# Places of tokens in a mixture of experts: reckoned from scores, by products and scans, with the softmax behind them

## The chip, the core and the metric

The kernel runs on one core of one Trainium2 chip. The time is the device time of one execution in microseconds (us); the number that counts is the median of several executions. Five engines work side by side, each through its own queue in order: PE (TensorE, matrix products; PEld is its loading of weights), DVE (VectorE), ACT (ScalarE), POOL (GpSimd) and SP (SyncE, which here issues most DMAs). SBUF is the on-chip memory of 128 partitions, PSUM the smaller one that PE writes, in banks of 512 fp32 numbers a partition.

## The reference, cut to what matters

Two layers on a batch of 4 images of 384 channels and 32 x 32 places (1024 tokens each). The first layer is a selective scan in four directions, and then a mixture of four experts of which each token uses two; the second is an attention of 8 heads and a two-layer network. The change is in the routing of the experts:

```python
def _L0_ffn_ref(x, gate_w, gate_b, w1, b1, w2, b2):
    scores = jnp.einsum('bsd,de->bse', x, gate_w) + gate_b
    probs = jax.nn.softmax(scores, axis=-1)
    topk_vals, topk_idx = jax.lax.top_k(probs, TOP_K)
    mask = jnp.sum(jax.nn.one_hot(topk_idx, NUM_EXPERTS, dtype=probs.dtype), axis=-2)
    masked = probs * mask
    masked = masked / (jnp.sum(masked, axis=-1, keepdims=True) + 1e-09)
    h = jax.nn.gelu(jnp.einsum('bsd,edh->ebsh', x, w1) + b1[:, None, None, :], approximate=False)
    y = jnp.einsum('ebsh,ehd->ebsd', h, w2) + b2[:, None, None, :]
    return jnp.einsum('bse,ebsd->bsd', masked, y)
```

The kernel computes for each token only its two experts. So it needs three things: the *place* of each token's copy in a list that is sorted by expert, the *expert* of each block of that list, and the *gate* (the weight) of each copy.

## The kernel before, in words

**Scan layer.** `scan_layer` goes over 32 units (image, direction, half of the places). For each, `chunk` works in groups: POOL multiplies inputs (L440), ACT makes decays by exp (L449), DVE scans along the places (`tensor_tensor_scan`, L454) and multiplies half of the results (L461), POOL the other half (L468), and PE sums over the states (L475, into `acc`). `project` prepares the next unit beside it (dt_ps L365, `mag` and `lnw` on POOL, L395 and L396). The inputs `dtr` come by DMA from SP's queue (L424). POOL and DVE work in turn on `bx`: six buffers.

**Tail.** When an image's scan is done, its tail is laid beside the scan of the next one. `tail_batch` runs `route`, `first_layer` (`experts`, `combine`, `prologue`) and `second_layer` (`attention`, `last_layers`). The route of image 0 stands by itself; those of images 1 and 2 are the steps `between` of the last layers of images 0 and 1 (L1198), and that of image 3 comes behind the scan (L1383). I call them routes 0 to 3. The tail has high priority at most spots.

**Route.** `spread` turns the tokens, sums the scores `sc` (128 tokens on partitions, 8 blocks of tokens, 4 experts: 128x32) and their statistics, and then calls `places` (L683). Behind it the 16 scatters (L697, indirect DMAs issued by POOL) put each token's row at its place `pos`; `experts` loads the number of the expert of each of 11 blocks into SP's register (L880) and then that expert's weights (L889, L897). The gates are read by `combine` alone (L977), behind all experts.

**`places` before** (L709 to L869), all on 128 partitions, with small operands in one PSUM bank (`area`, by the name `places` in the profile; `small` cuts pieces of it):

- softmax over 4 experts: maximum, difference, exp on ACT (L734), sum, reciprocal, two products (L732 to L738)
- for each pair of experts whether one's probability is above the other's, ties by number (L745 to L748), their sum `number` (L751); `chosen` (first, second; L754), `rank` (either; L755)
- the gates: probability times `rank`, sum, reciprocal, product (L756 to L761)
- two products on PE, with a triangle of ones (`before`) and with ones, count how many tokens ahead of each, and how many in all, chose an expert (L767, L768); a copy brings both from PSUM (L770), and seven adds in a row sum up the blocks (L774), an eighth the totals (L776)
- how many whole pairs of blocks and odd blocks each expert uses (L780 to L795, four adds in a row for where each begins), then the places (L798 to L840)
- the expert of each block, from comparisons of block numbers with where each expert begins (`later`, L846, to L866)
- the gates are picked with the places in one product and one reduction (L832 to L835) and copied (L868).

**The order.** The program is laid out by a planner: the framework simulates the engines' times, and each engine's queue gets its instructions in the order of that simulation, by priority and then by readiness. Nothing near the change is ordered by hand. Within one PSUM bank it keeps PE and DVE from working at once.

Of the kernel before, what the change touches and what calls it, by code (L numbers as in the profile page):

```python
# [12 lines left out]
ALU = mybir.AluOpType  # L13
# [102 lines left out]
class Body:  # L116
# [525 lines left out]
    def spread(self, b, x1, room):  # L642
# [38 lines left out]
        nc.vector.tensor_add(sc, sc, self.bg.unsqueeze(1).to_broadcast([P, MB, NE]))  # L681
# [27 lines left out]
    def places(self, sc, room):  # L709
# [18 lines left out]
        def over(v):  # L728
            return v.unsqueeze(2).to_broadcast([P, nt, NE])

        red, prob = small([P, nt]), small([P, nt, NE])
        nc.vector.tensor_reduce(red, sc, AX.X, ALU.max)  # L732
        nc.vector.tensor_sub(sc, sc, over(red))
        nc.scalar.activation(sc, sc, AF.Exp)  # L734
        nc.vector.tensor_reduce(red, sc, AX.X, ALU.add)
        nc.vector.reciprocal(red, red)
        nc.vector.tensor_mul(prob, sc, over(red))
        nc.vector.tensor_mul(sc, sc, over(red))  # L738

        shape = [P, nt, NE, NE]  # L740
        mine = sc.unsqueeze(3).to_broadcast(shape)
        other = prob.unsqueeze(2).to_broadcast(shape)
        above = room.tile(shape, "g_above", "g_above")
        same = small(shape)
        nc.vector.tensor_tensor(above, other, mine, op=ALU.is_gt)  # L745
        nc.vector.tensor_tensor(same, other, mine, op=ALU.is_equal)
        nc.vector.tensor_mul(same, same, self.lower.unsqueeze(1).to_broadcast(shape))
        nc.vector.tensor_add(above, above, same)  # L748
        rank = room.tile([P, nt, NE], "g_rank", "g_rank")
        number = small([P, nt, NE])  # L750
        nc.vector.tensor_reduce(number, above, AX.X, ALU.add)  # L751
        chosen = small([P, TOP, nt, NE])
        for k in range(TOP):
            nc.vector.tensor_scalar(chosen[:, k], number, float(k), None, op0=ALU.is_equal)  # L754
        nc.vector.tensor_scalar(rank, number, float(TOP), None, op0=ALU.is_lt)  # L755
        nc.vector.tensor_mul(prob, prob, rank)  # L756
        nc.vector.tensor_reduce(red, prob, AX.X, ALU.add)
        nc.vector.tensor_scalar_add(red, red, 1e-9)
        part = room.tile([P, nt], "g_red", "g_red")
        nc.vector.reciprocal(part, red)  # L760
        nc.vector.tensor_mul(sc, prob, over(part))  # L761


        ps = room.bank("p", "cnt_ps")
        n = nt * NE
        flat = rank.rearrange("p m e -> p (m e)")
        nc.tensor.matmul(ps[:, :n], self.before, flat, start=True, stop=True)  # L767
        nc.tensor.matmul(ps[:, n : 2 * n], self.ones, flat, start=True, stop=True)  # L768
        cnt = small([P, 2, nt, NE])
        nc.vector.tensor_copy(cnt.rearrange("p t m e -> p (t m e)"), ps[:, : 2 * n])  # L770
        run = room.tile([P, nt, NE], "g_run", "g_run")
        nc.vector.memset(run[:, 0, :], 0.0)
        for m in range(nt - 1):
            nc.vector.tensor_add(run[:, m + 1, :], run[:, m, :], cnt[:, 1, m, :])  # L774
        total = small([P, NE])
        nc.vector.tensor_add(total, run[:, nt - 1, :], cnt[:, 1, nt - 1, :])  # L776

        ns = nt * P // P
        need = room.tile([P, NE, ns], "g_need", "g_need")
        nc.vector.tensor_tensor(  # L780
            need, total.unsqueeze(2).to_broadcast([P, NE, ns]),
            self.full[:, :ns].unsqueeze(1).to_broadcast([P, NE, ns]), op=ALU.is_gt,
        )

        used = small([P, 2, NE])
        blocks = room.tile([P, NE], "g_blocks", "g_blocks")
        nc.vector.tensor_reduce(blocks, need, AX.X, ALU.add)
        nc.vector.tensor_reduce(used[:, 0], need[:, :, 1::2], AX.X, ALU.add)
        nc.vector.scalar_tensor_tensor(
            used[:, 1], used[:, 0], -2.0, blocks, op0=ALU.mult, op1=ALU.add  # L790
        )
        first = room.tile([P, 2, NE + 1], "g_first", "g_first")
        nc.vector.memset(first[:, :, :1], 0.0)
        for e in range(NE):
            nc.vector.tensor_add(first[:, :, e + 1], first[:, :, e], used[:, :, e])  # L795
        pairs, odd = first[:, 0], first[:, 1]
# [4 lines left out]
        at = cnt[:, 0]  # L801
        nc.vector.tensor_add(at, at, run[:, :nt, :])
        full, back = room.tile([P, NE], "g_full", "g_full"), small([P, NE])
        nc.vector.tensor_scalar(
            back, odd[:, :NE], float(NHALF) - 0.5, -float((NHALF + 2) * P), op0=ALU.is_gt, op1=ALU.mult
        )
        nc.vector.scalar_tensor_tensor(
            back, odd[:, :NE], float(P), back, op0=ALU.mult, op1=ALU.add
        )
        nc.vector.tensor_scalar(  # L810
            full, more.to_broadcast([P, NE]), float(SLOT), float(NFULL * SLOT),
            op0=ALU.mult, op1=ALU.add,
        )
        nc.vector.tensor_add(back, back, full)
        nc.vector.scalar_tensor_tensor(
            back, pairs[:, 1:], -float(SLOT), back, op0=ALU.mult, op1=ALU.add
        )
        nc.vector.tensor_scalar(full, used[:, 0], float(SLOT), None, op0=ALU.mult)
        ends = room.tile([P, nt, NE], "g_ends", "g_ends")
        nc.vector.tensor_tensor(  # L820
            ends, at, full.unsqueeze(1).to_broadcast([P, nt, NE]), op=ALU.is_ge
        )
# [652 lines left out]
```

## Time and profile before

| what | value |
|---|---|
| timed executions | 4278.92, 4278.86, 4291.83 us; median 4278.92 |
| the profiled execution | 4300.74 us; its span 4299.0 us, granted PE clock 0.865 |
| busy in the span | PE 77%, DVE 66%, ACT 59%, POOL 70% |
| route 0: L732 to L868 | 807.75 to 849.46 us |
| route 1 | 1731.29 to 1771.21 us |
| route 2 | 2737.95 to 2781.50 us |
| route 3 | 3483.17 to 3499.03 us |
| POOL's last work of the scan layer ends | 3458 us |

All times in a view of the profile count from the span's start. A row of a group or tile gives the line of the code, the engine, the operation, what it writes and reads, and durations in ns. A row of the waits gives who waited for whom, us in total, how often and the longest. A duration on DVE goes from the start of an instruction to its last write, so neighbours may overlap by some 0.1 us.

### The profile page before, as it was taken

How to read it: one execution, taken by the hardware profiler on the slowest of the kernel's cores; microseconds unless marked ns; L12 is line 12 of the kernel's file. 1: busy time of each engine (PE TensorE's matmuls, PEld its weight loads, DVE VectorE, ACT ScalarE, POOL GpSimd, SP SyncE). 2: the span in 40 equal slices, each digit the busy share in tenths (PEclk: the TensorE clock that was granted, in tenths of full speed). 3: DMA queues.
4: the chain of work that ended last, by engine and by line, in shares of the span. 5: the costliest groups of instructions: out<-in, count | busy, mean ns of one | idle time of the engine just before them, and what ended most of it. 6: DMA issues, size and time to landing. Idle time of an engine off the chain costs nothing. (4 is left out here: it accounts for less than half of the span.)

```text
span 4299.0 us, 45575 instructions
## 1 busy us (share of the span) xinstructions
PE 3329.5 (77%) x13244; PEld 1560.8 (36%) x13244; DVE 2852.0 (66%) x4200; ACT 2516.4 (59%) x4486; POOL 3020.0 (70%) x1471
## 2 busy tenths in 40 slices
PE   6445444389897888589985889579896889998896
PEld 2111111155553223145652223135553225566322
DVE  5998997878786867788786878878887820010101
ACT  5555545556665775666664777666665654343354
POOL 5999997898898968789898978888989810000100
PEclk8666666689998999589997999679998999999997
DMA  5454563577795535578886434558789243345100
GB/s 140 128 124 122 135 170 107 168 220 224 229 276 158 137 113 142 169 207 236 239 257 191 114 101 140 158 173 237 234 236 272 77 158 100 121 143 202 50 26 19
DMA packets 410322, 693.69 MB, mean 161 GB/s; under 512 B 51024, under 2 KB 209616, under 8 KB 410064
## 3 DMA queue, kind: packets, MB, share of 16 engines
q1 hardware_dynamic: 400752, 664.29, 53.4%
q0 software_dynamic: 8192, 25.17, 1.8%
q8 instruction: 106, 1.74, 0.2%
q14 instruction: 152, 1.25, 0.1%
q10 hardware_dynamic: 1120, 1.25, 0.1%
HBM read 569.00 MB, written 121.50 MB: 161 GB/s over the span
## 5 line engine op out<-in xcount | busy, mean ns | idle before, releaser
L440 POOL TENSOR_TENSOR bx<-dtr,bcs 128x1024 f32<-128x1024 f32 x768 | 1791.8, 2358 | 181.1 <-PE acc L475 93.6
L449 ACT ACTIVATE da<-dtr,nega 128x512 f32<-128x512 f32 x1536 | 1045.5, 690 | 928.7 <-DVE bx L461 580.8
L468 POOL TENSOR_TENSOR bx<-bx,bcs 128x1024 f32<-128x1024 f32 x384 | 903.7, 2357 | 154.6 <-DVE carry L465 67.3
L475 PE MATMUL acc<-bx,sel 128*32 128x512 f32 x3072 | 493.5, 701 | 306.4 <-POOL bx L468 261.0
L941 PE MATMUL h_ps<-xc,w 128*128 128x256 f32 (+1 forms) x3168 | 663.5, 365 | 47.7 <-DVE xc L928 17.4
L956 PE MATMUL y_ps<-w,hs 128*128 128x384 f32 x1824 | 644.6, 507 | 52.5 <-ACT hs L949 52.5
L941 PEld LDWEIGHTS h_ps<-xc,w 128*128 128x128 f32 x3168 | 551.2, 198 | 218.9 <-issue 93.7
L454 DVE TENSOR_TENSOR_SCAN bx<-da,carry,bx 128x512 f32<-128x512 f32 x384 | 473.8, 1270 | 114.7 <-ACT da L449 64.4
L454 DVE TENSOR_TENSOR_SCAN da<-da,carry,bx 128x512 f32<-128x512 f32 x384 | 476.1, 1273 | 77.5 <-ACT da L449 62.1
L454 DVE TENSOR_TENSOR_SCAN bx<-da,bx 128x512 f32<-128x512 f32 x384 | 453.7, 1211 | 90.9 <-ACT da L449 54.3
L461 DVE TENSOR_TENSOR bx<-da,bcs 128x512 f32<-128x512 f32 x768 | 509.8, 679 | 3.0
L454 DVE TENSOR_TENSOR_SCAN da<-da,bx 128x512 f32<-128x512 f32 x384 | 455.5, 1219 | 76.5 <-ACT da L449 53.0
L956 PEld LDWEIGHTS y_ps<-w,hs 128*128 128x128 f32 x1824 | 353.0, 197 | 337.4 <-issue 71.7
L1071 ACT ACTIVATE ex<-s_ps 128x512 f32<-128x512 f32 x512 | 300.3, 591 | 164.2 <-PE s_ps L1065 148.4
L1065 PE MATMUL s_ps<-w 64*128 64x512 f32 x1024 | 305.1, 659 | 68.5 <-ACT ex L1071 64.4
L977 POOL TENSOR_TENSOR diag<-ident,g_weight 128x1024 f32<-128x1024 f32 x8 | 15.1, 1903 | 443.1 <-PE xc_ps L924 430.0
L1111 PE MATMUL o_acc<-ex,vt 128*64 128x512 f32 x1024 | 286.1, 638 | 24.6 <-ACT ex L1071 18.5
L946 ACT ACTIVATE hs<-h_ps,bb 128x256 f32<-128x256 f32 (+1 forms) x528 | 199.9, 440 | 174.9 <-PE h_ps L941 170.9
L475 PEld LDWEIGHTS acc<-bx,sel 128*32 128x32 f32 x3072 | 76.2, 116 | 603.9 <-POOL bx L468 373.3
L960 DVE TENSOR_TENSOR y<-y_ps,bb 128x384 f32<-128x384 f32 x76 | 41.6, 548 | 250.6 <-PE y_ps L956 250.6
L365 PE MATMUL dt_ps<-xd,wdt 108*128 108x512 f32 x192 | 123.6, 731 | 73.0 <-ACT mag L404 48.3
L1065 PEld LDWEIGHTS s_ps<-w 64*128 64x128 f32 x1024 | 81.8, 189 | 269.1 <-ACT ex L1071 222.6
(218 smaller groups left out, 3593.3 us busy)
## 6 DMA issues: line engine op xcount, KB each, us to landing
w<-in_w SPq DMA_DIRECT2D x352, 576.0 KB
dtr<-dd SPq DMA_DIRECT2D x1536, 128.0 KB
bcs<-both SPq DMA_DIRECT2D x512, 128.0 KB
dd<-one_e SPq DMA_DIRECT2D x96, 256.0 KB
dd<-mag SPq DMA_DIRECT2D x96, 256.0 KB
rows<-zero SPq DMA_DIRECT2D x76, 192.0 KB
xt<-x SPq DMA_DIRECT2D x32, 384.0 KB
xs<-rows SPq DMA_DIRECT2D x32, 384.0 KB
```

What stands on the lines that cost most here:

```text
L440: pool = nc.gpsimd.tensor_mul(bx, dtr[q][1], bc[:, 0].unsqueeze(1).to_broadcast([P, 2, HF])).ins
L449: nc.scalar.activation(da, dtr[q][0][:, j, :], AF.Exp, scale=nega[:, col : col + 1])
L454: nc.vector.tensor_tensor_scan(run(h), run(da), run(bx[:, j, :]), 0.0 if first else hold, ALU.mult, ALU.add,)
L461: dve = nc.vector.tensor_mul(bx[:, j, :], h, cg).ins
L468: pool = nc.gpsimd.tensor_mul(bx, bx, cg.unsqueeze(1).to_broadcast([P, 2, HF])).ins
L475: nc.tensor.matmul(acc[lo : lo + DB, :], sel, out[q][:, j, :], start=(g == 0), stop=(g == NG - 1),)
L941: nc.tensor.matmul(ps[:, r, :], w1[(f + r) // wf][:, c, (f + r) % wf * P : ((f + r) % wf + 1) * P], xc[:, c, :], start=(c == 0), stop=(c = ...
L946: nc.scalar.activation(hs[:, f + r, :], ps[:, r, :], AF.Identity, bias=bb[:, f + r : f + r + 1])
L956: nc.tensor.matmul(out[:, :D], hs[:, f, t * P : (t + 1) * P], w2[f // wf][:, f % wf, :], start=(f == 0), stop=(f == FC - 1),)
L1065: ins = nc.tensor.matmul(ps, w[rows, j * P : (j + 1) * P], w[rows, halves(i)], start=True, stop=True).ins
L1071: done.append(nc.scalar.activation(ex[:, o, :], ps, AF.Exp, scale=HD**-0.5, accum_out=sums[:, t, 2 * j + o, i : i + 1],).ins)
L1111: ins = nc.tensor.matmul(out[cols, :], made[t][1][:, j, cols], ex[:, o, :], start=(j == 0), stop=(j == MB - 1),).ins
```

## The change

`spread` no longer adds the bias; `places` does. The order of probabilities is the order of the scores, so the comparisons take the scores, and everything that leads to places and experts comes first. The softmax and the gates stand at the end. Where the comparison needs two copies of the scores, one (`score`) is made in PSUM. The count by two products, a copy and nine adds becomes ten products that accumulate in PSUM: their first columns are the places within an expert, the last the totals. The adds in a row for where each expert begins become scans over 16 flags; the scan of the pairs is made twice, once into SBUF and once into PSUM (`again`). Several steps are joined, and several small pieces move between SBUF and PSUM.

```diff
-        nc.vector.tensor_add(sc, sc, self.bg.unsqueeze(1).to_broadcast([P, MB, NE]))
...
+        score = small([P, nt, NE])
+        nc.vector.tensor_add(score, sc, bg)
+        nc.vector.tensor_add(sc, sc, bg)
...
+        above = room.tile([P, nt, NE, 2, NE], "g_above", "g_above")
+        same = small(shape)
+        nc.vector.tensor_tensor(same, other, mine, op=ALU.is_equal)
+        nc.vector.tensor_tensor(above[:, :, :, 0], other, mine, op=ALU.is_gt)
+        nc.vector.tensor_mul(above[:, :, :, 1], same, self.lower.unsqueeze(1).to_broadcast(shape))
+        number = small([P, nt, NE])
+        nc.vector.tensor_reduce(
+            number, above.rearrange("p m e t o -> p m e (t o)"), AX.X, ALU.add
+        )
+        rank = room.tile([P, nt, NE], "g_rank", "g_rank")
+        nc.vector.tensor_scalar(rank, number, float(TOP), None, op0=ALU.is_lt)
+        at, total = small([P, nt, NE]), small([P, 1, NE])
+        lo = used_up[0] - (nt + 1) * NE
+        count = area[:, lo : used_up[0]].rearrange("p (m e) -> p m e", e=NE)
+        nc.tensor.matmul(count[:, 0, :], self.before, rank[:, 0, :], start=True, stop=True)
+        for m in range(nt):
+            nc.tensor.matmul(
+                count[:, m + 1 :, :], self.ones,
+                rank[:, m, :].unsqueeze(1).to_broadcast([P, nt - m, NE]),
+                start=(m == 0), stop=(m == nt - 1), skip_group_check=True,
+            )
+            if m == 0:
+                nc.tensor.matmul(
+                    count[:, 1:nt, :], self.before, rank[:, 1:, :],
+                    start=False, stop=False, skip_group_check=True,
+                )
...
+        need = small([P, 2, NE, nj])
+        nc.vector.tensor_tensor(need, total..., self.full..., op=ALU.is_gt)
+        pairs_sb = room.tile([P, 1 + NE * nj], "g_pairs", "g_pairs")
+        pairs_ps, blocks_ps = small([P, 1 + NE * nj]), small([P, 1 + NE * nj])
+        def sums(out, t):
+            nc.vector.memset(out[:, :1], 0.0)
+            nc.vector.tensor_tensor_scan(
+                out[:, 1:], self.ones[:, : NE * nj], need[:, t].rearrange("p e j -> p (e j)"),
+                0.0, ALU.mult, ALU.add,
+            )
+            return out[:, ::nj]
+        pairs, even = sums(pairs_sb, 1), sums(blocks_ps, 0)
+        odd = small([P, NE + 1])
+        nc.vector.tensor_sub(odd, even, pairs)
+        again = sums(pairs_ps, 1)
+        used = room.tile([P, NE], "g_used", "g_used")
+        nc.vector.tensor_reduce(used, need[:, 1], AX.X, ALU.add)
...
+        row = room.tile([P, nt, 2, NE], "g_row", "g_row")
...
+        chosen = small([P, TOP, nt, NE])
+        for k in range(TOP):
+            nc.vector.tensor_scalar(chosen[:, k], number, float(k), None, op0=ALU.is_equal)
+        picked = room.tile([P, TOP, nt, 2, NE], "g_pick", "g_pick")
+        for t in range(2):
+            nc.vector.tensor_mul(picked[:, :, :, t], chosen, row[:, :, t]...)
+        place = small([P, TOP, nt])
+        nc.vector.tensor_reduce(place..., picked..., AX.X, ALU.add)
+        pos = room.sb.tile([P, TOP, nt], I32, tag="g_pos", name="g_pos", bufs=2)
+        nc.vector.tensor_copy(pos, place)
...
+        ef = room.tile([P, NSLOT], "g_ef", "g_ef")
+        lone, both = later(NHALF, odd, "lone"), later(NFULL + 1, again, "later")
+        half = small([P, NHALF])
+        nc.vector.tensor_reduce(half, lone, AX.X, ALU.add)
+        nc.vector.tensor_reduce(ef[:, : NFULL + 1], both, AX.X, ALU.add)
+        other = room.tile([P, NHALF], "g_half", "g_half")
+        nc.vector.tensor_reduce(other[:, 2:], lone[:, : NHALF - 2], AX.X, ALU.add)
+        nc.vector.tensor_copy(other[:, :2], ef[:, NFULL : NFULL + 1].to_broadcast([P, 2]))
+        nc.vector.tensor_sub(other, other, half)
+        nc.vector.scalar_tensor_tensor(
+            ef[:, NFULL:], other, more, half, op0=ALU.mult, op1=ALU.add
+        )
+        expert = room.sb.tile([P, NSLOT], I32, tag="g_expert", name="g_expert", bufs=2)
+        nc.vector.tensor_copy(expert, ef)
...
         red, prob = small([P, nt]), small([P, nt, NE])
         nc.vector.tensor_reduce(red, sc, AX.X, ALU.max)
         nc.vector.tensor_sub(sc, sc, over(red))
...
+        gates = room.tile([P, TOP, nt, NE], "g_gates", "g_gates")
+        nc.vector.tensor_mul(gates, chosen, sc.unsqueeze(1).to_broadcast([P, TOP, nt, NE]))
+        weight = room.tile([P, TOP, nt], "g_weight", "g_weight")
+        nc.vector.tensor_reduce(weight..., gates..., AX.X, ALU.add)
```

Left out behind `row` are the three steps that fill it: the place in the expert's pairs, whether the token is in the expert's last odd block, and how far off that one lies. In this cut, a "..." within a line stands for the broadcast or rearranged view of the operand.

## The prediction

> **What bounds the kernel now.** I read the page first, for its slices, and then only the four places where `places` runs, since nothing else is edited.
>
> ```profile
> PE 3329.5 (77%) x13244; PEld 1560.8 (36%) x13244; DVE 2852.0 (66%) x4200; ACT 2516.4 (59%) x4486; POOL 3020.0 (70%) x1471
> ...
> PE   6445444389897888589985889579896889998896
> ...
> DVE  5998997878786867788786878878887820010101
> ...
> ```
>
> That fence's slices read so: up to about 3457 us the scan layer runs, and DVE and POOL are busy for seven tenths or more in nearly every slice (POOL's row, not shown, is like DVE's); behind it both are all but idle and PE is at nine tenths. (A slice is 107 us, so the scan fills the first 32.) The scan stage is paced by POOL's products (L440, L468) and the DVE scans between them; the tail by PE.
>
> The table by stretch, one row for each of the four routes, comes next; its columns are the stretch, its length, then busy us (count) of PE, PEld, DVE, ACT, POOL, the granted clock, DMA share and GB/s.
>
> ```profile
> 807.50:849.50 42.00, 9.28 (x38) 2.72 (x38) 40.08 (x100) 19.29 (x33) 23.29 (x11) 0.57 0.40 124
> 1731.00:1771.40 40.40, 23.04 (x74) 6.18 (x78) 35.37 (x99) 23.08 (x34) 27.87 (x13) 0.54 0.33 88
> 2733.50:2781.60 48.10, 21.32 (x58) 4.66 (x58) 43.35 (x98) 25.70 (x39) 36.48 (x17) 0.54 0.33 98
> 3482.60:3499.00 16.40, 13.19 (x73) 5.46 (x70) 11.69 (x68) 9.82 (x25) 0.00 (x0) 1.00 0.23 76
> ```
>
> In the first three DVE is busy 40.1 of 42.0, 35.4 of 40.4 and 43.4 of 48.1 us while POOL is busy only 23.3, 27.9 and 36.5. So for these 130 us of the scan DVE is the pacer and POOL, the pacer elsewhere, waits. The waits of POOL in three windows around them (route 0, 1, 2 in this order) name what it waited for:
>
> ```profile
> POOL bx L468 <- DVE places L754: 7.0, 1, 7.0
> POOL bx L468 <- DVE carry L465: 6.5, 1, 6.5
> ...
> POOL rows L697 <- DVE g_weight L868: 7.4, 1, 7.4
> ...
> POOL bx L468 <- DVE g_ends L823: 5.4, 1, 5.4
> ```
>
> With 2.3 us more for the positions in route 0 (L697) and 1.9 in route 2 (L735) these are 30.5 us in which POOL stood behind this code. That is the most that the change can win in the scan.
>
> Why DVE is slow there is seen in the views of the tiles `g_later`, `g_half`, `g_ef` and `g_full` (min/median/max ns over the four routes):
>
> ```profile
> L846 DVE TENSOR_TENSOR g_later<-slot_at_i,g_first x4: 178/1339/6737, 822.9 to 3495.5; 128x27 f32<-128x27 f32 x4
> L846 DVE TENSOR_TENSOR g_lone<-slot_at_i,g_first x4: 155/158/2358, 823.5 to 3495.6; 128x9 f32<-128x9 f32 x4
> L858 DVE TENSOR_TENSOR g_half<-g_ef,g_half x4: 144/150/2297, 829.4 to 3496.2; 128x2 f32<-128x2 f32 x4
> L861 DVE TENSOR_TENSOR g_half<-g_half x4: 141/153/2369, 831.6 to 3496.2; 128x1 f32<-128x1 f32 x4
> L862 DVE SCALAR_TENSOR_TENSOR g_ef<-g_half,g_more x4: 221/222/2246, 834.0 to 3496.4; 128x3 f32<-128x3 f32 x4
> L866 DVE CAST g_expert<-g_ef x4: 172/173/1198, 837.4 to 3496.7; 128x11 int32<-128x11 f32 x4
> L853 DVE TENSOR_REDUCE g_ef<-g_later x4: 165/166/169, 827.1 to 3495.9; 128x9 f32<-128x27 f32 x4
> ```
>
> Operations on one to 27 elements take 0.14 to 0.22 us when POOL rests and up to 2.4 us (once 6.74) while it multiplies. Only those stretch whose operands are all in SBUF; the reduction (L853), and every line with an operand in `places` (PSUM), keeps its time in all four routes.
>
> **The change, part by part.** Durations are those of one execution of 4300.74 us (span 4299.0); the three timed runs have a median of 4278.92 (to 4291.83), 0.5% below it. I work out differences and take them off the median.
>
> *Operands moved to PSUM.* The new `later` compares read `odd` and `again`, `half` and the last steps have a PSUM operand. Of the two-input lines stretched in routes 0 to 2, this takes L846 (0.69-0.18, 2.36-0.16, 6.74-0.18 and 1.99-0.18), L858 (2.30-0.15), L861 (2.37-0.15) and L862 (2.25-0.22): 0.51+2.20+6.56+1.81+2.15+2.22+2.03 = 17.5 us. The one-input stretches (L866 1.03, L810 0.84) I keep: the expert cast stays in SBUF and a copy of `ef` joins it. Added is one more add with both inputs in SBUF (`score`, its result in PSUM); no row has that form. Bounds: nothing, or 2.3 us each; I take the nearest rows, L680 and L681, which in routes 0 to 2 lost 2.00+1.15 us in six tries, 0.5 each, 1.6 for three. Net -15.9.
>
> The Trainium skill (SBUF — State Buffer, "Who interferes with whom") says that a DVE instruction with two SBUF inputs is blocked by a GpSimd instruction that reads SBUF; it names the inputs and not the result. By it `score` can lose like L846: 3 x 2.3 = 6.9 us rather than 1.6, and the net would be -10.6.
>
> *Fewer instructions.* Before, L681 and the body of `places` are 64 DVE instructions, whose unstretched durations (route 3) sum to 11.7 us; after it they are 51. Priced by the nearest rows: 0.19 for a 32-element step, 0.16 for a 4-element one, 0.29 for one of 128, a 256-element reduction 0.42, and three scans of 16 elements, which no row shows: between 0.16 (L774) and 1.21 (L454 on 512), near the small end, 0.19 (all three 0.5 to 3.6, taken 0.6). Sum 9.6, so -2.2 a route, -6.5 for three.
>
> The skill speaks against it (Perfetto Trace Analysis, "Optimizing Scalar/DVE Operations"): DVE pays about 60 ns to reach SBUF and 125 to reach PSUM, so some 15 steps moved to PSUM would cost 1 us a route. The trace has 0.15 for L804 with its result in PSUM against 0.144 to 0.150 for L858 in SBUF alone; I charge nothing.
>
> *Products for sums.* Two products, a copy (L770) and nine adds become ten accumulating products that leave positions and totals in PSUM. From the time view of route 0, then of route 3:
>
> ```profile
> 815.45 0.61 PE L767 MATMUL cnt_ps<-g_rank,before_i 128*128 128x32 f32 x2 [8.67 <-ACT da L449]
> ...
> 815.87 0.61 PE L768 MATMUL cnt_ps<-g_rank,ones 128*128 128x32 f32 x2
> ```
>
> A product is two instructions, and starts 0.42 us after the one before it (0.24 in route 3, at full clock, from 3490.54 to 3490.78). Eight more are 3.4 us of PE in routes 0 to 2, where PE is busy 9.3 of 42.0, 23.0 of 40.4 and 21.3 of 48.1 us and hides them, and 1.9 in route 3. But the step to `need` now waits for ten products (4.2+0.2 us) where L770 waited for two; behind `need` stand the scans (L454) for which POOL waits. If scans are queued ahead of `need`, as L454 was put between L757 and L758, the wait is free; if not it is 3.4 more. I take 1.0 a route: +3.0.
>
> *Softmax behind.* The 32-element exp (L734) now follows positions and experts. DVE waited for it 0.9, 3.7, 0 and 1.5 us. It still must wait, but for the gates, which only `combine` reads far later. Bounds -4.6 to +4.6 over three routes (an ACT queue deeper at the new spot); I take 0. The scatter (L697), and SP's load of expert numbers (L880, which held SP's queue up to 21.0 us in route 1), are released sooner; the 16 scatters a route still take POOL 1.27 us each (20 us), only sooner, in its queue before products that then come as much later; what queues behind L880 on SP are weights and `dtr` loads, and no wait of POOL in these windows names `dtr`, so I count nothing.
>
> *Route 3.* From L681 to L840 it takes 16.0 us (3482.95 to 3498.94). Without exp and its wait (2.8) and softmax steps the positions come 3 to 4 us sooner, less 1.8 for products. PE is busy 160.0 of the 160 us from 3540 and 149.4 of the next 150: attention of batch 2 fills what the scatter leaves, so 2 us sooner against 1.9 us of PE: 0. Were the cover gone, -4 to +2.
>
> *Sum.* DVE is freed of 15.9+6.5-3.0 = 19.4 us in the three routes, out of POOL's 30.5. Not all comes through: POOL also waited 7.6 us for `acc` (L475) in route 1, and DVE idles 1.9 to 5 us in each. I take three quarters, 15 us. Forecast 4279-15 = **4264 us**.
>
> **Rivals.**
>
> *Products become the wait (slower).* `need` goes straight behind `rank` in DVE's queue, and other PE work, such as the 3.63 us group at L1226, comes between the products, which share one PSUM tile with all DVE steps. DVE then stands 4.4 us and 3.6 for each such group in each of routes 0 to 2, and the scans queued behind it starve POOL. For it: PE's queue holds such groups in routes 1 and 2, at a clock of 0.54. Against: L770 waited 0.4 us at most. It decides from a stand of 7.5 us a route, where 3 x 7.5 eats the 22.4 us freed before products are counted; with two groups between, 4.4+7.3 = 11.7 us, it is 35.1-22.4 = 12.7 too much: **4292**.
>
> *The time freed is not on the path.* POOL's gaps fill with its other waits (L440 for `acc` 93.6 us, for `dtr` 31.0 over the scan), or the scan ends sooner and PE, left with the same attention work, ends when it did. For: PE's nine tenths behind 3457. Against: PE is idle half of each window. **4279**, 4268 to 4290.
>
> *All of it comes.* All 30.5 us of POOL's waits go: **4248**.
>
> *It doesn't do what it says.* The planner orders queues by its own estimate; if the softmax still goes ahead of the positions, only operand places and counts remain: 4264 to 4268, since I gave the softmax's move nothing in the scan; its chance is inside the forecast's.
>
> A new plan also shifts far loads and groups; I allow the spread of the three runs, 13 us, to each side.
>
> **How the numbers follow.** Forecast (4254 to 4272) 0.42, of which 0.32 is faster by over 0.3% (12.8 us, about what a measurement can tell); all of it 0.17; not on the path 0.17; products 0.24. So faster 0.49, same 0.10+0.17 = 0.27, slower 0.24. The range runs from 4240 to 4298: it holds the forecast, the quiet rival, most of both outer ones.
>
> **What would show it.** Right: in routes 0 to 2 no compare or half step above 0.3 us; the three windows shorter by 4 to 10 us, POOL's waits there under 15 us; the tenth product within 5 us of `rank`. Wrong: DVE idle before `need` for over 5 us; `score` stretched to 2 us each time; the windows shorter but the end of POOL's work (3457) unmoved, or that moved and the end not.

## The result, and the profile after

| | before | after |
|---|---|---|
| median (lowest to highest) | 4288.3 us (4278.86 to 4292.33, 6 runs) | 4264.31 us (4256.45 to 4270.68, 6 runs) |
| ratio, 95% interval | 1 | 0.9947 [0.9931, 0.9964] |
| span of the profiled execution | 4299.0 us | 4258.3 us |

The kernel is 24 us faster by the medians, 0.53% by the ratio on record. The forecast was 15 us (0.35%) and 4264. That the time is the one forecast, to 0.3 us, is luck: the kernel before measured 9 us longer here than in the three runs that the forecast started from, and the gain is 9 us more than forecast, and the two cancel.

The page of after, to be set beside the first fence of the prediction:

```profile
PE 3330.8 (78%) x13308; PEld 1572.8 (37%) x13308; DVE 2838.3 (67%) x4148; ACT 2519.7 (59%) x4486; POOL 3020.0 (71%) x1471
...
PE   6445544389887888689996888679986899998896
...
DVE  5999997788877877788877878778877830000101
```

PE has 64 instructions more (32 products, of two instructions each), DVE 52 fewer; the scan still fills 32 slices and PE's nine tenths stand behind it. The table by stretch, again one row for each route from the first step of `places` to the gates (columns: stretch, length, busy us (count) of PE, PEld, DVE, ACT, POOL, clock, DMA share, GB/s):

```profile
804.30:834.60 30.30, 13.87 (x48) 6.55 (x48) 28.46 (x82) 17.94 (x31) 21.33 (x15) 0.56 0.63 188
1718.50:1753.20 34.70, 20.34 (x82) 6.20 (x76) 30.23 (x87) 25.11 (x38) 30.92 (x16) 0.62 0.49 140
2704.00:2731.30 27.30, 18.97 (x68) 7.43 (x68) 20.23 (x61) 20.06 (x30) 14.79 (x12) 0.63 0.44 137
3470.50:3488.00 17.50, 16.56 (x66) 6.13 (x62) 9.01 (x52) 12.33 (x34) 4.51 (x5) 0.80 0.41 112
```

The first three are 11.7, 5.7 and 20.8 us shorter; the prediction asked for 4 to 10. The length of a window isn't the gain, though: in route 2 DVE has 23.1 us less to do in it, of which only 3.3 us are work of `places` (14.27 to 10.95 us); the rest is scan work that now lies outside. The waits of POOL in windows round the first three (waiter, whom it waited for, us in total, times, longest):

```profile
POOL bx L468 <- DVE carry L465: 4.9, 1, 4.9
...
POOL rows L696 <- DVE places L872: 0.2, 1, 0.2
...
POOL bx L468 <- DVE g_back L812: 0.9, 1, 0.9
...
POOL bx L468 <- DVE bx L454: 5.5, 1, 5.5
...
POOL rows L696 <- DVE places L875: 0.3, 1, 0.3
```

Of the 30.5 us that POOL stood behind this code (a `carry` of route 0 among them, 6.5) there are left 11.8: 1.4 us for the code itself, 4.9 us for that `carry`, and 5.5 us for scans of route 2 (L454) that are queued behind the first steps of `places`, which took 2.0 of these 5.5 us. The views of single tiles (min/median/max ns over the four routes) show why:

```profile
L849 DVE TENSOR_TENSOR g_later<-slot_at_i,places x4: 175/175/176, 820.4 to 3481.5; 128x27 f32<-128x27 f32 x4
L862 DVE COPY g_half<-g_ef x4: 144/544/1387, 823.1 to 3482.0; 128x2 f32<-128x2 f32 x4
L863 DVE TENSOR_TENSOR g_half<-g_half,places x4: 132/154/158, 823.2 to 3482.2; 128x3 f32<-128x3 f32 x4
L868 DVE CAST g_expert<-g_ef x4: 163/958/1836, 823.7 to 3482.6; 128x11 int32<-128x11 f32 x4
L733 DVE TENSOR_TENSOR places<-sc,bg x4: 193/195/2282, 804.6 to 3471.1; 128x32 f32<-128x32 f32 x4
```

The compare that had taken up to 6.74 us takes 0.176 at most (L849), the half step beside it 0.158 (L863). What still stretches has all its inputs in SBUF: the copy L862 (0.92 and 1.39 us in routes 1 and 2), the cast L868 (1.75 and 1.84 in routes 0 and 1) and, once, `score` (L733).

**Where the time went.** The scan layer's 32 units end in the same order in both kernels, so the ends of its units (each the end of the unit's last scan, L454) cut the span into comparable stages. Route 0 lies in the ninth unit, route 1 in the 17th and 18th, route 2 in the 19th to 26th. Rows for the ninth unit, the 10th to 16th, and all behind the scan, same columns as above, first of before:

```profile
751.80:888.00 136.20, 53.51 (x200) 24.01 (x197) 107.79 (x216) 61.56 (x100) 112.66 (x63) 0.63 0.58 182
888.00:1662.10 774.10, 679.15 (x2873) 333.15 (x2872) 605.54 (x815) 519.63 (x970) 663.18 (x317) 0.94 0.66 189
...
3435.20:4299.00 863.80, 778.87 (x3144) 387.35 (x3142) 89.20 (x230) 378.45 (x797) 38.38 (x37) 0.95 0.30 102
```

then of after:

```profile
751.10:875.50 124.40, 58.01 (x202) 27.88 (x199) 97.52 (x203) 62.37 (x100) 112.80 (x63) 0.63 0.65 195
875.50:1628.50 753.00, 651.48 (x2777) 318.41 (x2775) 601.35 (x807) 515.40 (x964) 660.35 (x316) 0.94 0.67 191
...
3421.80:4258.30 836.50, 759.56 (x3073) 386.48 (x3071) 88.23 (x217) 363.99 (x755) 39.40 (x38) 0.95 0.31 104
```

In the ninth unit POOL's work is the same (112.7 and 112.8 us) and DVE's is 10.3 us less: the unit is 11.8 us shorter. Here the change itself is at work. The two other rows are something else. No line of the change runs in units 10 to 16, yet they are 21.1 us shorter, and there PE has 96 instructions and 28 us less to do; behind the scan it has 71 instructions and 19 us less. This is work of the tail that has another place in PE's queue: units 17 to 26 hold it, and are 27.0 us *longer* (249.0+883.5 before, 258.7+900.8 after), although routes 1 and 2 in them are shorter. So of the 40.7 us between the two profiles, 11.8 stand in the ninth unit, and most of the rest in stages that differ in which tail work the planner put there. POOL's last work of the scan layer ends at 3445.0 us, 13.0 earlier than before. The experiments ask whether that order is a part of the change's effect or an accident of it.

### The profile page after: what moved, and what is told of

Its sections match the earlier page's. It is cut to its first block, busy times and chain, and to the rows that moved or that the text cites. A ratio compares the mean times of both kernels' runs of the same rounds, so it can differ in the third digit from the quotient of the medians.

```text
span 4258.3 us, 45670 instructions
## 1 busy us (share of the span) xinstructions
PE 3330.8 (78%) x13308; PEld 1572.8 (37%) x13308; DVE 2838.3 (67%) x4148; ACT 2519.7 (59%) x4486; POOL 3020.0 (71%) x1471
## 3 DMA queue, kind: packets, MB, share of 16 engines
q8 instruction: 107, 1.75, 0.2%
## 5 line engine op out<-in xcount | busy, mean ns | idle before, releaser
L440 POOL TENSOR_TENSOR bx<-dtr,bcs 128x1024 f32<-128x1024 f32 x768 | 1793.7, 2362 | 195.6 <-PE acc L475 84.0
L468 POOL TENSOR_TENSOR bx<-bx,bcs 128x1024 f32<-128x1024 f32 x384 | 905.4, 2362 | 132.4 <-DVE carry L465 59.9
L978 PE MATMUL y_ps<-w,hs 128*128 128x384 f32 x1824 | 643.7, 506 | 55.9 <-ACT hs L971 54.9
L454 DVE TENSOR_TENSOR_SCAN bx<-da,carry,bx 128x512 f32<-128x512 f32 x384 | 473.7, 1271 | 134.5 <-POOL bx L440 69.5
L454 DVE TENSOR_TENSOR_SCAN bx<-da,bx 128x512 f32<-128x512 f32 x384 | 452.3, 1210 | 125.4 <-POOL bx L440 69.7
L454 DVE TENSOR_TENSOR_SCAN da<-da,carry,bx 128x512 f32<-128x512 f32 x384 | 475.7, 1274 | 79.5 <-ACT da L449 63.1
L454 DVE TENSOR_TENSOR_SCAN da<-da,bx 128x512 f32<-128x512 f32 x384 | 455.4, 1219 | 67.5 <-ACT da L449 46.8
```

The costliest lines, as they stand in the source:

```text
L440: pool = nc.gpsimd.tensor_mul(bx, dtr[q][1], bc[:, 0].unsqueeze(1).to_broadcast([P, 2, HF])).ins
L454: nc.vector.tensor_tensor_scan(run(h), run(da), run(bx[:, j, :]), 0.0 if first else hold, ALU.mult, ALU.add,)
L468: pool = nc.gpsimd.tensor_mul(bx, bx, cg.unsqueeze(1).to_broadcast([P, 2, HF])).ins
L978: nc.tensor.matmul(out[:, :D], hs[:, f, t * P : (t + 1) * P], w2[f // wf][:, f % wf, :], start=(f == 0), stop=(f == FC - 1),)
```

## The experiments

Four theories are named in the expectations. **S**: what counts are the DVE instructions stretched by POOL, and their end. **N**: fewer instructions and fewer waits. **E**: positions and experts are ready earlier, the softmax being behind. **P**: any edit gives the planner another order of all queues, and that order moves the time. All ratios are to runs of the kernel before on the same chip; after itself was not run again beside the later kernels, so it is compared with them by these ratios.

Since stages can be compared where totals mislead, here are all kernels by stage (us of the profiled execution; units counted from 1) ahead of the single verdicts. Each row is one execution, and stages of one execution scatter: up to 1740 us the queues of PE, ACT and POOL have the same order in before and b_ctl, and (but for the place of one exp on ACT) the same in after, a_ctl2, a_one, a_two and a_blk, yet units 10 to 16 took 774.1 and 781.3 us, and 753.0 to 764.2.

| kernel | ratio, 95% interval | unit 9 (route 0) | 10–16 | 17–18 (route 1) | 19–26 (route 2) | 27–32 | behind the scan |
|---|---|---|---|---|---|---|---|
| before | 1 | 136.2 | 774.1 | 249.0 | 883.5 | 640.6 | 863.8 |
| b_ctl | 1.0063 [1.0044, 1.0081] | 136.2 | 781.3 | 241.5 | 916.1 | 634.4 | 854.8 |
| b_ctl4 | 1.0044 [1.0027, 1.0061] | 134.5 | 772.9 | 240.1 | 914.4 | 636.0 | 861.9 |
| after | 0.9947 [0.9931, 0.9964] | 124.4 | 753.0 | 258.7 | 900.8 | 633.8 | 836.5 |
| a_ctl | 0.9980 [0.9965, 0.9995] | 128.3 | 760.7 | 258.9 | 919.9 | 624.9 | 836.8 |
| a_ctl2 | 0.9996 [0.9987, 1.0006] | 124.2 | 758.4 | 260.2 | 909.8 | 642.8 | 845.9 |
| b_psum | 0.9932 [0.9914, 0.9951] | 128.4 | 758.2 | 244.4 | 873.5 | 643.4 | 855.9 |
| a_sbuf | 0.9955 [0.9937, 0.9973] | 126.6 | 761.0 | 252.2 | 883.3 | 642.8 | 848.7 |
| a_prod | 1.0047 [1.0032, 1.0062] | 130.8 | 766.2 | 253.5 | 892.1 | 648.2 | 868.0 |
| a_smfirst | 1.0051 [1.0038, 1.0065] | 129.6 | 767.2 | 261.9 | 908.7 | 632.7 | 858.1 |
| a_free | 1.0064 [1.0044, 1.0085] | 126.7 | 754.4 | 256.1 | 925.9 | 642.5 | 864.8 |
| a_blk | 0.9978 [0.9967, 0.9990] | 127.3 | 764.2 | 274.9 | 923.7 | 624.2 | 823.1 |
| a_one | 0.9965 [0.9949, 0.9980] | 125.5 | 758.5 | 272.6 | 922.6 | 623.8 | 826.8 |
| a_two | 0.9985 [0.9974, 0.9996] | 131.0 | 757.7 | 272.8 | 926.4 | 625.9 | 829.1 |

**b_psum: the operands alone.** Before, with the compares' and half steps' operands in PSUM, for which the two differences of the half steps become a reduction, a copy and one difference; nothing else of the change.

```diff
+        again = small([P, 2, NE + 1])
+        nc.vector.tensor_copy(again, first)
...
-            ef[:, : NFULL + 1], later(NFULL + 1, pairs, "later"), AX.X, ALU.add
+            ef[:, : NFULL + 1], later(NFULL + 1, again[:, 0], "later"), AX.X, ALU.add
...
-        half = room.tile([P, 2, NHALF], "g_half", "g_half")
...
+        half = small([P, NHALF])
+        lone = later(NHALF, again[:, 1], "lone")
```

> The kernel before with one part of the change alone: the comparisons and half sums of `later` get an operand in PSUM (two more DVE instructions a route). Theory S (what was won is DVE time lost to operations whose inputs all lie in SBUF while POOL works): the stretched rows of L846, L858, L861, L862 vanish (17.5 us in three routes), time 9 to 15 us below the kernel before, ratio 0.9965 to 0.998. Theory N (fewer and earlier instructions won it): no gain, ratio 0.999 to 1.001. Theory P (what was won comes from the new order of the queues that the planner lays out): any ratio from 0.995 to 1.005, without regard to the stretched rows.

Measured 4258.5 us (4252.53 to 4270.18), beside 4290.1 for before. The tile's view:

```profile
L848 DVE TENSOR_TENSOR g_later<-slot_at_i,places x4: 170/171/172, 837.2 to 3459.6; 128x27 f32<-128x27 f32 x4
```

The compare has lost its stretch in all four routes, with POOL as busy as ever. The ninth unit is 6 to 8 us shorter than with the three orders of before, and this at nearly the same order: PE's, ACT's and POOL's queues are those of before up to its 874 us, and DVE's differs only in how the steps of `places` lie between its other work. DVE spent 12.7 us from L681 on in route 0, where it had spent 22.5. POOL still waits 7.0 us in route 0 for L754, the step behind the softmax. As a whole this kernel can't be told from after (the intervals overlap), with none of the products, scans or the move of the softmax.

**a_sbuf: the operands back.** After, with the starts of the experts, `odd` and `half` in SBUF again (and, not in this cut, `wrap` in PSUM).

```diff
-        odd = small([P, NE + 1])
+        odd = room.tile([P, NE + 1], "g_odd", "g_odd")
...
-        lone, both = later(NHALF, odd, "lone"), later(NFULL + 1, again, "later")
-        half = small([P, NHALF])
+        lone, both = later(NHALF, odd, "lone"), later(NFULL + 1, pairs, "later")
+        half = room.tile([P, NHALF], "g_hsum", "g_hsum")
```

> The changed kernel with those operands back in SBUF (`odd`, `half` and the compared starts; same number of instructions). Theory S: the stretched rows are back, 9 to 15 us above the changed kernel, so ratio to the kernel before 0.9965 to 0.998. Theory N: as fast as the changed kernel, 0.994 to 0.996. Theory P: anywhere from 0.990 to 1.000.

Measured 4268.4 us (4262.14 to 4279.82).

```profile
L863 DVE TENSOR_TENSOR g_half<-g_half,g_hsum x4: 145/237/1859, 818.1 to 3471.1; 128x3 f32<-128x3 f32 x4
L864 DVE SCALAR_TENSOR_TENSOR g_ef<-g_half,g_more,g_hsum x4: 205/704/2265, 820.0 to 3471.3; 128x3 f32<-128x3 f32 x4
```

The stretch is back: the time above 0.45 us of each instruction from L680 on sums over routes 0 to 2 to 17.8 us here, against 6.7 in after and 19.4 in before. But no price of it shows. The ratio is what theory N expected and below theory S's range, which its interval reaches; from after's it can't be told (0.9955 against 0.9947). The ninth unit is 2.2 us longer than in after, which is within the 124.2 to 128.3 us of after's three orders.

**b_ctl and a_ctl: the same instructions in another order.** In before the two lines that make `chosen` go behind `rank` (the diff); in after they go up behind `rank` from their place ahead of `picked`.

```diff
+        nc.vector.tensor_scalar(rank, number, float(TOP), None, op0=ALU.is_lt)
...
-        nc.vector.tensor_scalar(rank, number, float(TOP), None, op0=ALU.is_lt)
```

> A control: the kernel before with the two lines of `chosen` moved behind the line of `rank`; the same instructions with the same operands, but another plan of all queues. Theories S and N: within 0.2% of the kernel before. Theory P: off by 0.3% or more, either way.

> A control: the changed kernel with the two lines of `chosen` moved up behind `rank`, ahead of the ten products; the same instructions with the same operands, but another plan. Theories S and N: within 0.2% of the changed kernel, ratio to the kernel before 0.993 to 0.997. Theory P: off from that by 0.3% or more, either way.

Measured 4319.15 us (4311.43 to 4322.09) and 4284.26 us (4272.95 to 4292.73), beside 4290.1. An exchange that changes no work costs before 0.63% and after 0.33%. In the traces, 3993 of PE's 13244 places and 339 of POOL's 1471 hold something else in b_ctl than in before, and 5644 of 13308 and 385 of 1471 in a_ctl than in after. The ninth units move by 0 and 3.9 us; most of what moves is behind.

**a_free and a_blk: twenty more compares a route,** in after, with one operand in PSUM and with both in SBUF.

```diff
+        extra = room.tile([P, NFULL + 1, NE - 1], "g_extra", "g_extra")
+        for _ in range(20):
+            nc.vector.tensor_tensor(extra, self.slot_at..., again[:, 1:NE]..., op=ALU.is_ge)
```

(`pairs` in place of `again` in a_blk.)

> The changed kernel with 20 more comparisons of 27 elements a route ahead of the positions, each with one input in PSUM and one in SBUF; their results are not used. They take 0.17 us each and stretch in no route: 20 x 0.17 x 3 = 10 us more DVE time in routes 0 to 2. Theories S and N: 5 to 10 us above the changed kernel. The two controls so far show that a new plan by itself can add or take 15 to 30 us, so theory P allows from 10 below to 40 above.

> The same 20 comparisons a route, but with both inputs in SBUF; their results are not used. Theory S: where POOL works they stretch, by 0.5 us (the rate of L680 and L681 before) to 1.2 us (the mean of the other two-input rows) each over 60 of them in routes 0 to 2: 30 to 70 us of DVE time more than the kernel with a PSUM input, of which three quarters, 25 to 55 us, is seen in the time. Theory P (the stretched rows do not matter, the order of the queues does): within 30 us of the kernel with a PSUM input, either way, and POOL's waits in the routes no longer.

Measured 4320.02 and 4286.62 us, beside 4294.71 (4288.65 to 4310.28). The instructions did what theory S says: all 80 took 0.155 to 0.183 us in a_free, while in a_blk the twenty of routes 0, 1 and 2 took 10.5, 11.5 and 6.8 us in place of 3.6. But the kernel with the stretched ones was the *faster*, by 33 us. Every theory missed: a_free is 1.17% above after by the ratios, 50 us, where theory P had allowed 40, and a_blk lies 33 us below a_free, where S had said 25 to 55 above and P within 30. The orders of the queues differ between the two, so the pair prices nothing; it shows that the order can outweigh 18 us of stretched DVE work.

**a_prod: the ten products made three times,** the first two sets into a place that nobody reads.

```diff
+        extra = small([P, nt + 1, NE])
+        for _ in range(2):
+            nc.tensor.matmul(extra[:, 0, :], self.before, rank[:, 0, :], start=True, stop=True)
...
```

> The changed kernel with the ten products made three times (the second and third set into unused columns of the same bank): 20 more products a route, 8.4 us of PE at 0.42 each, between `rank` and `need`. If DVE has scans to do meanwhile (the forecast's case) routes 0 to 2 cost nothing and route 3 under 5 us: within 5 us of the changed kernel but for a new plan. If products are the wait (the rival): 3 x 8.4 = 25 us more, and DVE idle ahead of `need` for 8 us or more a route.

Measured 4313.73 us. `need` now comes 13.05, 13.05 and 16.96 us behind `rank` in routes 0 to 2, and the time view of route 0 on DVE shows what it does meanwhile (start, duration, idle time before and its releaser in brackets):

```profile
809.32 2.33 DVE L454 TENSOR_TENSOR_SCAN bx<-da,bx 128x512 f32<-128x512 f32 x2
...
812.93 2.33 DVE L454 TENSOR_TENSOR_SCAN da<-da,bx 128x512 f32<-128x512 f32 x2
...
822.45 0.20 DVE L784 TENSOR_TENSOR places<-places,full_i 128x32 f32<-128x32 f32 x1 [0.98 <-PE places L770]
```

Scans are queued ahead of `need`, and it stands 0.98, 0.42 and 0 us for even thirty products (in route 0 it had also stood 3.42 us for POOL's `lnw`, ahead of L402). Only in route 3, where no scan is left, does DVE stand all 12.79 us. The ninth unit is 6.4 us longer than in after and 2.5 longer than in the longest of after's three orders. The total, 43 us above after by the ratios, holds a new order and prices nothing.

**a_smfirst: softmax and gate quotients ahead of the products again,** the rest of after kept.

```diff
+        ex = room.tile([P, nt, NE], "g_ex", "g_ex")
...
+        nc.scalar.activation(ex, ex, AF.Exp)
...
-        nc.scalar.activation(sc, sc, AF.Exp)
```

> The changed kernel with the softmax and the gates' quotients ahead of the products again (the comparisons still take scores; same instructions, exp into a tile of its own). Positions then come later by the 12 steps and the wait for ACT, 2 to 6 us a route. My prediction gave the softmax's place nothing: within 5 us of the changed kernel but for a new plan. A theory that says the early positions won the time (theory E): 10 us or more above the changed kernel, with POOL waiting for positions again.

Measured 4315.19 us. The positions come 26.2 us behind `rank` in route 0 (11.9 in after), and POOL stands 7.1 us for `rank` again, as it stood 7.0 for L754 in before. For the positions themselves it doesn't wait in that window. The ninth unit is 5.2 us longer than in after, 1.3 longer than the longest of after's three orders. The total is 45 us above after by the ratios, as theory E had asked (10 or more), but that of a_prod, which leaves the softmax behind, is 43 above; and b_psum, with the softmax in front, is as fast as after.

**a_one and a_two: stretch at one order.** This pair mends what was wrong with the last one. Twenty instructions a route on 17 elements of SBUF, in a_one with one input (a reduction), in a_two with two. All queues of PE, ACT, POOL and SP have the same order in both, and DVE's differs in these 80 instructions and in one exchange of a memset of 0.06 us with a scan.

```diff
+        extra = room.tile([P, 1 + NE * nj], "g_extra", "g_extra")
+        for _ in range(20):
+            nc.vector.tensor_reduce(extra, pairs_sb.unsqueeze(2), AX.X, ALU.add)      (a_one)
+            nc.vector.tensor_tensor(extra, pairs_sb, pairs_sb, op=ALU.add)            (a_two)
```

> The kernel after with twenty additions to each route behind the scans of `need`, each a one-input reduction of 17 elements from SBUF into SBUF, their result read by nobody (80 in all). It is the partner of the next run, which has twenty two-input adds of the same 17 elements in the same places; every engine's queue is otherwise in the same order in both, so the two differ in nothing but the form of these 80 instructions. All theories: each reduction 0.14 to 0.18 us, 3 to 3.6 us a route, none over 0.5 us. Theory P (the order of the queues decides): the time against the kernel before lies anywhere from 4255 to 4325, since the order is a new one. It has no meaning by itself.

> The same with twenty two-input adds of 17 elements, all operands in SBUF, in place of the reductions. Theory S (stretched instructions cost the time of the scan): in routes 0 to 2 the twenty take 6 to 12 us each route instead of 3.3, about 18 us more in all, and the kernel is 9 to 18 us slower than its partner (0.2 to 0.4%). Theory off-path (DVE's lost time is hidden): the twenty stretch the same, but the kernel is within 5 us of its partner (0.1%).

Measured 4283.32 us (4274.18 to 4296.70, 9 runs) and 4293.41 us (4287.77 to 4301.88, 12 runs). The tile, first of a_one, then of a_two:

```profile
L799 DVE TENSOR_REDUCE g_extra<-g_pairs x80: 147/165/175, 811.0 to 3510.5; 128x17 f32<-128x17 f32 x80
```

```profile
L799 DVE TENSOR_TENSOR g_extra<-g_pairs x80: 146/172/2283, 810.3 to 3522.3; 128x17 f32<-128x17 f32 x80
```

The medians agree (0.165 and 0.172 us), the maxima don't: against POOL some of the two-input adds take 2.28 us. In routes 0 to 2 the twenty take 3.30, 3.27 and 3.34 us in a_one and 11.19, 11.43 and 6.43 in a_two, 19.1 us more in all. The scan ends 10.1 us later (3460.4 against 3450.3), and the median is 10.1 us higher (ratio 1.0024, 95% interval 1.0002 to 1.0041 by resampling the runs). So stretch does reach the end, about half of it by the medians: theory S, at the lower edge of what it expected. How much is not known well: the interval is 1 to 18 us, and its lower part is what the theory that DVE's lost time is hidden allowed (5).

a_blk is a third kernel of this order: its queues of PE, ACT and POOL are those of a_one and a_two, SP's differs in one exchange, DVE's besides the 80 instructions in places of route 0. Its twenty took 18.8 us more than those of a_one, and its ratio is 0.13% higher, 6 us, though from another chip.

**b_ctl4 and a_ctl2: two more orders.** In before the compares for "above" and "equal" are exchanged; in after the two calls of `later`.

```diff
-        lone, both = later(NHALF, odd, "lone"), later(NFULL + 1, again, "later")
+        both, lone = later(NFULL + 1, again, "later"), later(NHALF, odd, "lone")
```

> Control: the kernel before with two neighbouring lines of the comparison exchanged (the one for above, the one for equal), which does the same work with the same instructions; a quarter of PE's queue comes out in another order. Theory P: it differs from the kernel before by 5 to 30 us, either way, as the first control (4319 against 4290) did. Theories S and N: within 5 us of the kernel before.

> Control: the kernel after with the two calls of `later` exchanged, the same instructions in another order; only a tenth of PE's queue behind route 0 comes out in another order. Theory P: 4255 to 4295, that is up to 30 us from the kernel after (4264), with the same end of the eighth scan unit (874 to 882 us) as all others with the change. Theories S and N: within 5 us of 4264.

(The unit called the eighth there is the ninth of the table.) Measured 4317.39 us (4311.46 to 4326.81) and 4297.55 us (4292.93 to 4306.06), beside 4301.3. The ninth unit of a_ctl2 ends at 876.0 us and is as long as after's (124.2 and 124.4), but the kernel as a whole has lost all that after had gained, and the interval holds 1. PE's, ACT's and POOL's orders in it differ from after's only behind 2745 us. Theory P is shown on both sides, for before directly, for after by ratios across chips.

**What the table says together.** Three orders of before have ninth units of 134.5 to 136.2 us, three orders of after 124.2 to 128.3: 10.0 us between the means, and no overlap. All other kernels that hold the change or a part of it have 125.5 to 131.0, those with twenty DVE instructions more among them. So this gain belongs to the change. The three of a side are here nearly repetitions of one order, since up to the end of this unit an exchange moves little more than the steps of `places`. Which part of the change makes the gain isn't settled. The end of the stretch suffices (b_psum). But DVE's time alone doesn't tell the unit's length: a_blk, with 22.9 us of it from L680 on in route 0, needs 127.3 us, and b_ctl4, also with 22.9, 134.5. Over the totals the three ratios of before are 1, 1.0044 and 1.0063, those of after 0.9947, 0.9980 and 0.9996: 0.61% between the means, again with no overlap, but each side scatters over 0.5 to 0.6%, which gives the difference of the means a standard error of 0.24% (from the scatter of three and three). It is 2.6 such errors; for 95% three and three need 2.8. The pair of the result, before against after, is the fastest of each three and has 0.53%.

## Why the prediction was right, point by point

**The bound** was read rightly: where `places` runs, DVE paced the scan, and when its instructions shrank, the waits of POOL behind it went from 30.5 to 11.8 us (forecast: under 15).

**Operands moved to PSUM (net −15.9).** Right in mechanism. The DVE time of L681 and `places` in routes 0 to 2 falls from 22.52+18.15+14.27 = 54.9 us to 13.37+12.08+10.95 = 36.4, that is by 18.5 where the two steps together said 22.4. The shares: unstretched (route 3) 11.74 to 9.85, so 5.7 for three routes, and the remaining 12.8 are stretch, not 15.9. The term that was mis-sized is what was left to stretch: I kept 1.9 us for one-input steps and added 1.6 for `score`. Measured were 3.2 us of lost time at the cast, 2.0 at the copy, and 2.1 for `score` in one of three tries. That is 7.3 us where I had 3.5; I charged nothing for the new copy L862.

On `score` the trace sides with the rule of the Trainium skill in kind: two SBUF inputs suffice, with the result in PSUM (2.28 us). In size it is nearer to my 1.6 than to the rule's 6.9, since only one of three met POOL; over the ten kernels with this step 11 of 30 tries in routes 0 to 2 were stretched, and it lost 1.9 us a kernel. The same page (SBUF — State Buffer, "SBUF: two separate sides") says more than I took from it: an fp32 copy from SBUF to SBUF works in a mode with two ports and so contends with GpSimd too. The copy (0.92 and 1.39 us) agrees with that, and the cast (up to 1.84) does likewise; the one-element L796, also SBUF alone, stayed at 0.148 to 0.150.

**Fewer instructions (−6.5).** Right: 5.7 (the prediction's own 11.7 less 9.6 is 2.1 a route, 6.3 for three). A scan of 16 elements took 0.17 to 0.195 us against the estimate of 0.19, the reduction of 256 took 0.428 against 0.42. Of the higher price for PSUM that the skill gives (Perfetto Trace Analysis, "Optimizing Scalar/DVE Operations") nothing is seen: compares with a PSUM operand take 0.155 (L849 on 9), those before with SBUF operands 0.155 where they aren't stretched (L846 on 9).

**Products for sums (+3.0).** The queue was priced rightly, 4.5 us from `rank` to the end of the tenth product in route 0, 4.9 and 5.5 in routes 1 and 2 (the sign asked for 5). The wait was priced too high: 0.9 us in route 0, none in routes 1 and 2. The time view of after, route 0:

```profile
808.51 0.19 DVE L748 TENSOR_SCALAR g_rank<-places 128x32 f32<-128x32 f32 x1
808.62 2.33 DVE L454 TENSOR_TENSOR_SCAN bx<-da,bx 128x512 f32<-128x512 f32 x2
...
813.22 0.20 DVE L770 TENSOR_TENSOR places<-places,full_i 128x32 f32<-128x32 f32 x1 [0.90 <-PE places L756]
```

Two scans went ahead of `need`, as the prediction had hoped. The slower rival, which decides from a stand of 7.5 us a route, falls with this, and with thirty products too (a_prod).

**Softmax behind (0).** Nearly right. DVE stands as long for the exp as it did, only at another spot: 0, 0.3 and 4.1 us in routes 0 to 2, where before had 0.9, 3.7 and 0. Both kernels that keep the softmax in front (b_psum, a_smfirst) have a wait of POOL of 7 us in route 0, where after, a_ctl2 and a_ctl have one of 4.9, 4.9 and 5.5 us for a `carry`: some 2 us, inside the bounds. Their ninth units (128.4 and 129.6) are at or just above the longest with the softmax behind (a_ctl, 128.3). In routes 1 and 2 the runs don't separate it from the order.

**Route 3 (0).** From the first step to the positions it takes 10.4 us where it took 16.0, 5.6 us less where the prediction had 2. Its 2.8 us for the exp and its wait aren't in its rows: DVE stood 1.5 us for L734. Its 1.8 us for the products were 4.1, since DVE has no scan left there and stood 4.5 us for them, where it had stood 0.4. The scatter starts 60.5 us behind the end of the scan against 64.5 before. Whether this reaches the end wasn't isolated: the stage behind the scan differs by the PE work that is left (836.5 us with 759.6 of PE, 863.8 with 778.9).

**Three quarters come through.** This was a choice, and the runs neither confirm nor refute it. At one order 10.1 of 19.1 us reached the end, a little over half, but with an interval from a twentieth to nine tenths. In the ninth unit it was 7.8 of 9.8 us for b_psum against before, 5.5 of 7.9 for a_two against a_one, and 1.8 of 7.2 for a_blk against a_one. For the change itself that unit is 11.8 us shorter where DVE was freed of 9.2; behind it no stage shows what routes 1 and 2 gave, since units 17 to 26 are 27.0 us longer. The rival in which all of it comes fails: it needs all 30.5 us of waits gone and 31 us of gain; 18.7 us of waits went, and the interval of the ratio, 0.36 to 0.69%, is 15 to 30 us.

**The order (13 us to each side).** This is the allowance that was too small. Exchanges of lines that change no work moved before by 19 and 27 us and after by 14 and 21 us (the ratios' differences times 4290). What the runs pin down for the mechanism is about 10 us in the ninth unit; whether the other 14 of the 24 came by it or by the order that the planner found isn't shown, and that the sum hit 4264 may owe something to that order. With a_ctl2's order the same change would have read "no difference". How much of the 0.61% between the two families is the change and how much the draw of the orders stays open; more orders on each side would be needed, or a program whose queues are held fixed, and neither was tried.

## What to carry to other kernels

Look for instructions of a few elements that take 1 to 2 us now and then: if both their inputs lie in SBUF while GpSimd works, one input in PSUM takes the stretch away (all 80 compares of a_free stayed under 0.19 us), and that edit alone (b_psum, in the one order that it was run in) gave as much as the whole rewrite could be shown to give. Where a planner lays out the queues, every edit is also a new draw of the order: measure two or three harmless exchanges of lines on each side, and compare stages that lie ahead of the first difference elsewhere, before a few tenths of a per cent are put down to an idea.

## What was not expected of the hardware

- A stretched instruction mostly lasts no longer than one product of POOL: 2.28 us at most among the 80 adds of a_two, while POOL's products on 1024 elements take 2.33 to 2.36 us (L440 and L468 in after, 800 to 860 us). L680 lasted 3.24 us in route 0 of b_psum, and one compare of before 6.74 us, nearly three products.
- A result in PSUM doesn't protect an instruction with two SBUF inputs (`score`, 2.28 us once in after), and one with one input can stretch as well (cast 1.84, copy 1.39), but not each: 80 reductions of SBUF on 17 elements stayed at 0.147 to 0.175 beside the same POOL work.
- DVE lost 19.1 us more in a_two than in a_one, and the scan, which DVE and POOL pace, ended only 10.1 later; in route 1, with 8.2 us of it, units 17 and 18 grew by 0.2 us (272.6 to 272.8).
